# Strassen blocks of keys and queries finished in PSUM, an output in another PSUM ring, weight sums on another engine: a two-layer gated model on one Trainium2 core

## The chip, the core and the metric

The kernel runs on one core of a Trainium2 chip. The metric is device time in microseconds (us). The engines have short names: PE is TensorE (matmuls and transposes), DVE is VectorE, ACT is ScalarE, POOL is GpSimd, and SP issues most of the DMAs. Each engine works through its own instructions in order. All data is float32.

## What is computed

Eight sequences of 256 tokens and 1024 features go through two layers. Each layer is a cross-attention and a feed-forward part, each added to x through a gate:

```python
x = x + tanh(g_xattn[0]) * autocorrelation(layernorm(x), ctx, ctx)
x = x + tanh(g_ffn[0])   * lora_ffn(layernorm(x), ...)      # the LoRA rank is chosen per token
x = x + tanh(g_xattn[1]) * attention(layernorm(x), ctx, ctx, mask, wq, wk, wv, wo)
x = x + tanh(g_ffn[1])   * fourier_ffn(layernorm(x), ...)   # W_base and an update from Fourier coefficients

def rope(x):                       # on queries and keys, 128 features of a head
    x1, x2 = x[..., :64], x[..., 64:]
    return x * cos + concat([-x2, x1]) * sin

def autocorrelation(Q, K, V):      # 8 heads of 128 features
    corr = ifft(fft(q) * conj(fft(k))).real
    w, idx = top_k(corr, int(2 * log(256)));  w = softmax(w)
    return sum(w[i] * v[min(idx[i] + pos, 255)] for i in range(topk))
```

The attention has 32 query heads on 8 key and value heads of 128 features.

## The kernel before

**Passes and stages.** Two passes of four sequences run one after another. A pass has four stages: the first layer's autocorrelation, its LoRA feed-forward part, the second layer's attention and its Fourier feed-forward part. The keys and values of the attention depend on the context alone, so their projection (`keys_values`) runs beside the autocorrelation: the generator `fill` takes its next steps at chosen places, so that PE has matmuls while other engines work on spectra. In the first pass the folding of the last layer's weights stands there too. A scheduler decides the final order on each engine.

**Seven products.** Matrix products are made by the Strassen-Winograd scheme: 7 products of half-size blocks in the order `SEVEN = (1, 2, 6, 7, 4, 5, 3)`, where operands are sums made beforehand (`left_operands`, `right_operands`) and results are combined. For keys, values and queries `combine` (L221 to L257) does that as each product ends in a PSUM tile of 128 x 512: product 1 is copied to `u` by ACT; 2 plus u is the first finished block (L229); 6 is added into u (L232); 7 plus u is `w` (L235); w minus 4 is a block (L254); 5 plus w is a block and 5 is added into u; 3 plus u is the last block (L250). For product 5 there are two forms. With `alone` (queries of the second pass) DVE makes both sums from PSUM (L238, L239). Otherwise ACT copies the product to `m` (L243), and POOL adds it into u (L244) and makes the block (L246). A finished block lies in SBUF: `c` for a key, `qT` for a query, `v` for a value.

**Rope.** A finished key or query is turned by `rope` (L718 to L728): DVE multiplies the two halves crosswise by the sine into a temporary tile (L725, L726), and the whole by the cosine (L727), and POOL adds the two (L728). The temporary tile "rope" has one buffer, so the next rope's first multiply waits for the add. Queries are turned in place; keys go from c into the tile that a DMA writes to the keys in DRAM.

**PSUM rings.** Beside the autocorrelation these are `ps_kv`, two tiles for the products of keys and values; `ps_dft`, four for spectra; one each for the correlation and for `ps_out`. The last holds the two transposes `pt` of a turn and the two outputs `po` (L540), one after another. Each po gets two matmuls (L542) and is added to x by two residuals on DVE (L381). A turn of the autocorrelation (a sequence's half of the features) makes spectra, multiplies them on DVE from PSUM (L438 to L441), adds the products on POOL (L442, L444), finds the largest lags (L584 to L598), and finishes the turn before. POOL makes the next turn's sums of tokens (L471 to L474), after which DVE corrects `ke` (L477). In the attention the query products (L987), the output products (L1017 in the first pass, L1080 in the second) and nothing else share the four tiles of `ps_mm`.

**Attention.** A step is one block of two sequences and one key head with its four query heads. Queries of the next step, scores, values and outputs are interleaved. In the first pass the outputs use seven products (`outputs`, L1017). In its block 1, at each second head, `finer_weights` makes from the weights of two heads the sums that the second pass needs: for each of seven operands two subtractions on DVE (L933, L934), two on POOL (L935, L936), and two DMAs to DRAM, from three buffers of "fine". The second pass takes two heads together (`outputs_of_two`) with 49 quarter-size products; POOL makes their left operands `oI` (L1059), and `stream_wo` loads the weights through a ring of seven big tiles.

**Big tiles.** Three groups of seven tiles of 4 KB per partition, "a", "b" and "xn", are shared by the stages; which of a and b is `ga` and `gb` alternates between passes. `before_fourier` prepares the Fourier part's first operands (norm, transposes, sums) near the end of the attention: six tiles, in ga, which is also the ring of the wo stream. `stored_weight` (L196) places 14 half weights: the first seven in the first group, the others in the second. For the Fourier part these are gb and "xn". The next pass's context blocks `cx` and their sums (POOL, L155 and L159) lie in one of the big groups too.

Of the kernel before, what the change touches and what calls it, by code (L numbers as in the profile page):

```python
# [19 lines left out]
P = 128  # L20
# [26 lines left out]
def flamingo_kernel(ctx: ExitStack, tc: tile.TileContext, a: dict, out: bass.AP):  # L47
# [147 lines left out]

    def stored_weight(groups, where):  # L196

        ops = {}
        for n, r in enumerate(SEVEN):
            ops[r] = Halves([groups[(2 * n + i) // 7] for i in range(2)], f"w_{r}")  # L200
            ops[r].load(where(r))
        return ops

# [14 lines left out]
        eng.tensor_sub(t4, t2, q[1][0])  # L218
        return {1: q[0][0], 2: q[1][0], 3: q[1][1], 4: t4, 5: t1, 6: t2, 7: q[0][1]}

    def combine(r, ps, tiles, new, dest, alone=False):  # L221


        if r == 1:
            tiles["u"] = new("u")
            nc.scalar.copy(tiles["u"], ps)
        elif r == 2:
            c = dest()
            nc.vector.tensor_add(c, ps, tiles["u"])  # L229
            return c, (0, 0)  # L230
        elif r == 6:
            nc.vector.tensor_add(tiles["u"], ps, tiles["u"])  # L232
        elif r == 7:
            tiles["w"] = new("w")
            nc.vector.tensor_add(tiles["w"], ps, tiles["u"])  # L235
        elif r == 5 and alone:
            c = dest()
            nc.vector.tensor_add(c, ps, tiles["w"])  # L238
            nc.vector.tensor_add(tiles["u"], ps, tiles["u"])  # L239
            return c, (1, 1)  # L240
        elif r == 5:
            m = new("m")
            nc.scalar.copy(m, ps)  # L243
            nc.gpsimd.tensor_add(tiles["u"], tiles["u"], m)  # L244
            c = dest()
            nc.gpsimd.tensor_add(c, tiles["w"], m)  # L246
            return c, (1, 1)
        elif r == 3:
            c = dest()
            nc.vector.tensor_add(c, ps, tiles["u"])  # L250
            return c, (0, 1)
        elif r == 4:
            c = dest()
            nc.vector.tensor_sub(c, tiles["w"], ps)  # L254
            return c, (1, 0)
        return None

    def add_product(r, ps, x, g, ng, part):

# [134 lines left out]
    def autocorrelation(p, xt, pools, beside, late):  # L394
# [88 lines left out]
        def turn(this, before, coming):  # L483


            after = None
            if this:
                b, cols, end, qe, qo, ke, ko = this
                if coming:
                    coming = loads(coming)  # L490
                kr_ps, ki_ps = dft((KCE, ke)), dft((KSE, ko), (NYQ, ke))


                kr, ki, kn = sb("kr"), sb("ki"), sb("kn")
                nc.scalar.copy(kr, kr_ps)
                nc.scalar.copy(kn, kr_ps)
                nc.scalar.activation(ki, ki_ps, AF.Copy, scale=pair)
                nc.scalar.copy(kn[0:1, :], ki_ps[0:1, :])
                re, im = sb("re"), sb("im")
                products(spectrum((CE, SE), (qe, qo)), kr, ki, kn, re, im, False)  # L500
                fill(2)

            if this:
                vr_ps, vi_ps = dft((KCO, ko)), dft((KSO, ke))
                vr, vi = sb("vr"), sb("vi")
                nc.scalar.copy(vr, vr_ps)
                nc.scalar.copy(vi, vi_ps)

                nc.vector.scalar_tensor_tensor(
                    kr[0:1, :], end[0:1, :], 2.0 * S, kr[0:1, :], ALU.mult, ALU.add  # L510
                )
                fill((1 if p == 0 else 2) if before else 6 if p == 0 else 2)
            last = not this
            if before:
                if last:
                    fill(3)
                b_cols, b_tiles, (bkr, bki, bkn, bvr, bvi, both) = before

# [12 lines left out]
                products(spectrum((CO, SO), wt[::-1]), bvr, bvi, bvr, odr, odi, True)  # L531
                fill(3 if last else 2)
            if this and coming:
                after = sums(*coming)

            def back(l):


                if before:
                    po = ps_out.tile([P, HALF], F32, tag="out", name="po")  # L540
                    for i, (k, sp) in enumerate(((0, er), (3, odi)) if l else ((1, ei), (2, odr))):
                        nc.tensor.matmul(po, inv2[:, k, :], sp, start=(i == 0), stop=(i == 1))  # L542
                    residual(b_tiles[0][:, b_cols], po, tg_x[0])
                    residual(b_tiles[1][:, b_cols], po, tg_x[0] if l else ntg_x[0])
                    fill(1 - l)

            if last:
                back(0)
                back(1)
                return None, None  # L550
            w = big_tile("xn", [4, S], "w")
            cor = correlation(re, im, 0)
            fill(1)
            back(0)
# [175 lines left out]
    def keys_values(n, groups, pools, tab):  # L730
# [61 lines left out]
        for u in range(4):  # L792
# [4 lines left out]
            for r in SEVEN:  # L797
                ps = ps_kv.tile([P, 2, S], F32, tag="kv", name=f"ps_{kind[1]}")
                for l in range(2):
# [9 lines left out]
                        )  # L809
                    if l == 0:  # L810
                        yield
                out_tile = lambda: w2.tile([P, 2, S], F32, tag="kv", name=kind[1])
                dest = (lambda: new("c")) if kind == "wk" else out_tile
                done = combine(r, ps, tiles, new, dest)
                if done:
                    c, (i, j) = done
                    if kind == "wk":
                        kT = out_tile()
                        rope(kT, c, tab[:, 0, :], tab[:, 1, :], w1)
                        place = kT_d.rearrange("(q l i) p t -> q i p l t", l=2, i=2)  # L820
                        nc.sync.dma_start(
                            place[i_u, i, :, :, t0 + j * S : t0 + (j + 1) * S], kT
                        )
                    else:
                        r0, c0 = t0 + j * S, i_u * HALF + i * S
                        nc.sync.dma_start(
                            v_d[r0 : r0 + S, c0 : c0 + S].rearrange("(t p) d -> p t d", p=P), c
                        )
# [33 lines left out]
    def attention(p, xt, gq, go, keep, norms, xops, ahead):  # L862
        with (
# [59 lines left out]
            def finer_weights(step):  # L923

                blk, g = step
                for n, r in enumerate(SEVEN):
# [3 lines left out]
                        w1.tile([P, 2, 2, S], F32, tag="fine", name=f"fine_{i}", bufs=3)  # L930
                        for i in ("t67", "t45")
                    )
                    nc.vector.tensor_sub(t45[:, 1], q[0][1], q[0][0])  # L933
                    nc.vector.tensor_sub(t67[:, 1], q[1][1], q[0][1])  # L934
                    nc.gpsimd.tensor_sub(t67[:, 0], q[1][1], t45[:, 1])  # L935
                    nc.gpsimd.tensor_sub(t45[:, 0], t67[:, 0], q[1][0])  # L936
                    nc.sync.dma_start(wo2_d[g // 2][:, n, 0], t67)
# [41 lines left out]
            def queries(step, qT):  # L979
# [3 lines left out]
                for r in SEVEN:  # L983
                    ps = ps_mm.tile([P, 2, S], F32, tag="mm", name="ps_q")
                    for l in range(2):
                        for c in range(KH):
# [4 lines left out]
                                start=(c == 0),  # L991
                                stop=(c == KH - 1),
                            )
                    new, dest = (lambda tag: half(tag, 1)), (lambda: half("qT", 7))
                    done = combine(r, ps, tiles, new, dest, paired)
                    if done:
                        qT[done[1]] = done[0]
                        rope(done[0], done[0], tab_q[:, 0, :], tab_q[:, 1, :], w1)
                    yield

            def outputs(step, ops):
# [359 lines left out]
    for p in range(NPASS):  # L1361
# [42 lines left out]
        with tc.tile_pool(name="at_keep", bufs=1, reuse_waits="tile") as kp:  # L1404
# [26 lines left out]
            def before_fourier(ps_t, tag):  # L1431
                norm = norm_stats(xt[:2])
                tiles = []
                for t in range(2):
                    xn = big_tile(ga, [D], "xn")
                    normed(xn, xt[t], *norm, t)
                    tiles.append(big_tile(ga, [KC, P], "xnT"))
                    transposed(tiles[t], xn, ps_t, tag)
                q = [[s[:, k * KH : (k + 1) * KH, :] for k in range(2)] for s in tiles]
                both = big_tile(ga, [2, KH, P], "s12")  # L1440
                s = both[:, 0], both[:, 1], big_tile(ga, [KH, P], "s4")
                first.update(left_operands(nc.vector, q, *s))

            attention(p, xt, gb, ga, keep, norms, xops, before_fourier)
        fourier_ffn(p, xt, (gb, "xn"), first)

# [136 lines left out]
```

## Time and profile before

| | us |
|---|---|
| median of three runs | 3379.02 |
| lowest and highest | 3375.74, 3380.23 |
| the profiled execution's own time | 3388.48 |
| its span | 3386.4 |

The granted TensorE clock is 0.99 over the span. The stages are told by the lines that run in them; cutting the span there gives this table of time, busy time of each engine with the number of instructions, granted clock, DMA share and GB/s:

```profile
core 0: us, PE busy (x) PEld busy (x) DVE busy (x) ACT busy (x) POOL busy (x), PEclk, DMA share, GB/s
0.00:100.00 100.00, 81.71 (x312) 63.99 (x313) 74.18 (x134) 20.06 (x34) 42.35 (x36) 0.95 0.70 257
100.00:395.00 295.00, 281.95 (x1060) 195.32 (x1060) 213.58 (x529) 85.71 (x156) 166.27 (x129) 0.99 0.42 137
395.00:548.00 153.00, 144.51 (x492) 74.70 (x491) 100.30 (x216) 19.79 (x40) 22.33 (x16) 0.97 0.38 139
548.00:1150.00 602.00, 597.74 (x2458) 438.60 (x2457) 460.33 (x725) 163.02 (x438) 247.27 (x234) 1.00 0.40 140
1150.00:1640.00 490.00, 474.51 (x1836) 329.59 (x1835) 363.71 (x572) 133.43 (x350) 280.39 (x240) 0.99 0.50 173
1640.00:1742.00 102.00, 101.42 (x273) 47.35 (x271) 55.00 (x85) 12.67 (x22) 38.11 (x29) 1.00 0.33 119
1742.00:2100.00 358.00, 340.94 (x1320) 248.72 (x1321) 259.39 (x609) 101.03 (x182) 176.59 (x136) 0.97 0.43 141
2100.00:2243.00 143.00, 140.55 (x499) 75.84 (x499) 73.65 (x186) 20.00 (x40) 22.97 (x20) 0.99 0.23 71
2243.00:3284.00 1041.00, 1022.52 (x4954) 889.64 (x4953) 768.33 (x1436) 292.16 (x795) 550.99 (x589) 1.00 0.51 165
3284.00:3386.00 102.00, 97.22 (x263) 45.53 (x261) 45.25 (x68) 10.28 (x18) 23.59 (x19) 0.99 0.10 41
```

From above: the start and the rest of the first pass's autocorrelation with keys and values; its LoRA part; block 0 and block 1 of its attention; its Fourier part; then the four stages of the second pass (autocorrelation with keys and values, LoRA, attention, Fourier). Records of matmuls overlap a little, and their ends are modelled, so a stage's PE time can look fuller than PE is.

In the lists of groups a row reads: line, engine, operation, out<-in by the program's names, shapes, count | busy us, mean ns of one | idle time of the engine just before them with what ended most of it. In the timelines a row reads: start us, duration us, engine, line, operation, out<-in, shapes, count [idle before <-releaser].

### The profile page before, as it was taken

To read this page: it belongs to the slowest core of one execution; us is meant where nothing else is said; L and a number is where in the kernel's file an instruction comes from. 1 tells how busy PE (TensorE), PEld (TensorE's weight loads), DVE (VectorE), ACT (ScalarE), POOL (GpSimd) and SP (SyncE) were. 2 spreads that over 40 slices of the span, in tenths; PEclk is the share of its full clock that TensorE was granted. 3 is DMA by queue.
4 is the path that set the end of the run, shared out by engine and by line. 5 is a ranking of instruction groups with operands and counts; after the bars stand their busy time and mean duration, and the time that the engine had idled before them with its cause. 6 is when DMAs were issued, how large, how long until landed. Compare 5 with 4: busy or idle time off the path is not lost. (4 is left out here: it accounts for less than half of the span.)

```text
span 3386.4 us, 39800 instructions
## 1 busy us (share of the span) xinstructions
PE 3283.1 (97%) x13456; PEld 2409.3 (71%) x13456; DVE 2413.7 (71%) x4553; ACT 858.2 (25%) x2075; POOL 1570.9 (46%) x1445
## 2 busy tenths in 40 slices
PE   8899999999999999999999999999999999999999
PEld 6666556777777766775456767568888888888864
DVE  7787656877777787677648775467777777777773
ACT  1333111322232322222113321113222222222310
POOL 4655212434443465466535552113564554554662
PEclk9999999999999999999999999999999999999999
DMA  7433625333333454564253434043454455555641
GB/s 270 171 116 110 217 96 177 119 135 133 136 128 132 133 204 144 177 225 169 81 196 125 141 105 162 7 157 103 161 183 157 155 167 172 165 165 179 207 140 50
DMA packets 215783, 505.56 MB, mean 149 GB/s; under 512 B 25076, under 2 KB 102900, under 8 KB 215582
## 3 DMA queue, kind: packets, MB, share of 16 engines
q1 hardware_dynamic: 214430, 498.84, 43.7%
q0 software_dynamic: 1152, 4.19, 0.3%
q8 instruction: 107, 1.75, 0.2%
q14 instruction: 94, 0.77, 0.1%
HBM read 394.96 MB, written 108.00 MB: 149 GB/s over the span
## 5 line engine op out<-in xcount | busy, mean ns | idle before, releaser
L728 POOL TENSOR_TENSOR qT<-qT,rope 128x512 f32<-128x512 f32 x128 | 169.5, 1324 | 675.2 <-DVE qT L727 675.2
L987 PE MATMUL ps_q<-xn,wq 128*128 128x256 f32 x1920 | 429.2, 379 | 2.7 <-DVE x L381 2.7
L987 PEld LDWEIGHTS ps_q<-xn,wq 128*128 128x128 f32 x1920 | 364.5, 190 | 54.3 <-DVE x L381 3.9
L1158 ACT ACTIVATE s<-s,nmx 128x256 f32<-128x256 f32 x512 | 255.9, 500 | 351.1 <-DVE nmx L1155 350.3
L1153 DVE COPY_PREDICATED s<-keep,ps_s 128x512 f32<-128x512 uint8 x256 | 185.4, 728 | 147.6 <-PE ps_s L1144 141.5
L987 PE MATMUL ps_q<-xn_t,wq 128*128 128x256 f32 x1280 | 285.6, 379 | 0.0
L987 PEld LDWEIGHTS ps_q<-xn_t,wq 128*128 128x128 f32 x1280 | 243.2, 190 | 33.1
L381 DVE SCALAR_TENSOR_TENSOR x<-po,tg,x 128x512 f32<-128x512 f32 x248 | 178.3, 744 | 121.5 <-PE po L1332 43.5
L1190 PE MATMUL av<-wT,v 128*128 128x256 f32 x1024 | 248.5, 386 | 13.7 <-ACT wT L1185 13.7
L1167 DVE TENSOR_SCALAR s<-s,tot 128x256 f32<-128x256 f32 x512 | 245.7, 520 | 7.1
L1144 PE MATMUL ps_s<-kT,qT 128*128 128x256 f32 x1024 | 249.6, 381 | 0.0
L1190 PEld LDWEIGHTS av<-wT,v 128*128 128x128 f32 x1024 | 193.3, 191 | 68.6 <-ACT wT L1185 24.2
L1080 PE MATMUL po<-wo,oI 128*128 128x256 f32 x896 | 218.6, 383 | 12.4 <-POOL oI L1059 8.3
L1185 ACT COPY wT<-pt 128x512 f32<-128x512 f32 x256 | 138.5, 588 | 361.3 <-PE pt L1179 360.9
L1144 PEld LDWEIGHTS ps_s<-kT,qT 128*128 128x128 f32 x1024 | 193.6, 192 | 26.3 <-issue 0.7
L1017 PE MATMUL po<-wo,oT 128*128 128x512 f32 x448 | 201.8, 593 | 0.0
L1080 PEld LDWEIGHTS po<-wo,oI 128*128 128x128 f32 x896 | 167.6, 191 | 44.8 <-POOL oI L1059 11.8
L1152 POOL MEMSET s<- 128x512 f32 x256 | 128.4, 527 | 141.2 <-PE pt L1179 133.7
L1155 DVE TENSOR_REDUCE nmx<-s 128x2 f32<-128x512 f32 x256 | 174.1, 683 | 6.9
L1080 PE MATMUL po<-wo,oT 128*128 128x256 f32 x672 | 168.7, 381 | 4.0 <-DVE co L1095 2.0
L1198 ACT COPY oT<-av 128x512 f32<-128x512 f32 x128 | 74.9, 585 | 362.9 <-PE av L1190 361.3
L264 POOL TENSOR_TENSOR x<-x,part 128x512 f32<-128x512 f32 x48 | 69.0, 1438 | 206.5 <-ACT part L263 206.4
(296 smaller groups left out, 6519.1 us busy)
## 6 DMA issues: line engine op xcount, KB each, us to landing
wo<-wo_d SPq DMA_DIRECT2D x144, 512.0 KB, 4.6
wq<-in_wq_dram SPq DMA_DIRECT2D x104, 512.0 KB, 3.5
wq<-wq_d SPq DMA_DIRECT2D x96, 512.0 KB, 3.3
wo<-in_wo_dram SPq DMA_DIRECT2D x56, 512.0 KB, 3.9
wo_d<-fine_t SPq DMA_DIRECT2D x56, 512.0 KB, 3.4
wo<-wo_d SPq DMA_DIRECT2D x96, 256.0 KB, 3.4
w<-w_d SPq DMA_DIRECT2D x36, 512.0 KB, 5.4
wo<-in_wo_dram SPq DMA_DIRECT2D x72, 256.0 KB, 3.3
```

What stands on the lines that cost most here:

```text
L381: nc.vector.scalar_tensor_tensor(xs, ps, g, xs, ALU.mult, ALU.add)
L728: nc.gpsimd.tensor_add(dst, dst, t)
L987: nc.tensor.matmul(ps[:, l, :], wops[r][:, l, c, :], xo[r][:, c, :], start=(c == 0), stop=(c == KH - 1),)
L1017: nc.tensor.matmul(po, ops[r][:, h, t * P : (t + 1) * P], wops[r][:, h, :], start=(h == 0), stop=(h == 1),)
L1080: nc.tensor.matmul(po, left[r2][:, h, :], w[:, h, :], start=(h == 0), stop=(h == 1))
L1144: nc.tensor.matmul(ps[:, t, :], qT[i, n][:, l, t * P : (t + 1) * P], kT[:, n * S : (n + 1) * S], start=True, stop=True,)
L1153: nc.vector.copy_predicated(s, keep[b], ps)
L1155: nc.vector.tensor_reduce(nmx, s, AX.X, ALU.max, negate=True)
L1158: nc.scalar.activation(s[:, t, :], s[:, t, :], AF.Exp, bias=nmx[:, t : t + 1], accum_out=tot[:, t : t + 1],)
L1167: nc.vector.tensor_scalar(s[:, t, :], s[:, t, :], tot[:, t : t + 1], None, ALU.mult)
L1185: nc.scalar.copy(wT[i], pt)
L1190: nc.tensor.matmul(av[:, i, :], kv[step][1][:, n * 2 + c, :], wT[i][:, c, :], start=(c == 0), stop=(c == 1),)
```

## The change

1. A finished block of a key or query is written back into the PSUM tile of its product: `combine` gets the tile through `dest(ps)`, and for keys and queries `dest` returns that tile. Rope's three multiplies then read PSUM. A query's result goes into a new `qT` tile; values still go to SBUF.
2. Product 5 has one form: DVE adds it into u, and then makes the block. ACT's copy m and POOL's two additions are gone (32 products: 16 of queries in the first pass, 8 of keys, 8 of values).
3. The autocorrelation's outputs po take tiles of the spectra's ring `ps_dft` instead of `ps_out`.
4. In `finer_weights` the first two subtractions are POOL's too, so all four are.
5. `before_fourier` takes its six tiles from "xn" instead of ga, and the Fourier part's 14 half weights lie in three groups: seven in gb, three in "xn", four in ga. With two groups, as in the LoRA part, the same rule gives the places of before.

```diff
     def stored_weight(groups, where):
         ops = {}
+        place = [groups[0]] * 7 + [groups[1]] * 3 + [groups[-1]] * 4
         for n, r in enumerate(SEVEN):
-            ops[r] = Halves([groups[(2 * n + i) // 7] for i in range(2)], f"w_{r}")
+            ops[r] = Halves(place[2 * n : 2 * n + 2], f"w_{r}")
             ops[r].load(where(r))
         return ops
...
-    def combine(r, ps, tiles, new, dest, alone=False):
+    def combine(r, ps, tiles, new, dest):
         if r == 1:
             tiles["u"] = new("u")
             nc.scalar.copy(tiles["u"], ps)
...
-        elif r == 5 and alone:
-            c = dest()
-            nc.vector.tensor_add(c, ps, tiles["w"])
-            nc.vector.tensor_add(tiles["u"], ps, tiles["u"])
-            return c, (1, 1)
-        elif r == 5:
-            m = new("m")
-            nc.scalar.copy(m, ps)
-            nc.gpsimd.tensor_add(tiles["u"], tiles["u"], m)
-            c = dest()
-            nc.gpsimd.tensor_add(c, tiles["w"], m)
-            return c, (1, 1)
...
+            return None
+        u = tiles["u"]
+        if r == 6:
+            nc.vector.tensor_add(u, ps, u)
+            return None
+        if r == 7:
+            tiles["w"] = new("w")
+            nc.vector.tensor_add(tiles["w"], ps, u)
+            return None
+        if r == 5:
+            nc.vector.tensor_add(u, ps, u)
+        c = dest(ps)
+        if r == 4:
+            nc.vector.tensor_sub(c, tiles["w"], ps)
+        else:
+            nc.vector.tensor_add(c, ps, tiles["w"] if r == 5 else u)
+        return c, {2: (0, 0), 5: (1, 1), 3: (0, 1), 4: (1, 0)}[r]
...
                 if before:
-                    po = ps_out.tile([P, HALF], F32, tag="out", name="po")
+                    po = ps_dft.tile([P, HALF], F32, tag="dft", name="po")
...
-                out_tile = lambda: w2.tile([P, 2, S], F32, tag="kv", name=kind[1])
-                dest = (lambda: new("c")) if kind == "wk" else out_tile
-                done = combine(r, ps, tiles, new, dest)
+                out_tile = lambda _: w2.tile([P, 2, S], F32, tag="kv", name=kind[1])
+                done = combine(r, ps, tiles, new, (lambda ps: ps) if kind == "wk" else out_tile)
...
-                    nc.vector.tensor_sub(t45[:, 1], q[0][1], q[0][0])
-                    nc.vector.tensor_sub(t67[:, 1], q[1][1], q[0][1])
+                    nc.gpsimd.tensor_sub(t45[:, 1], q[0][1], q[0][0])
+                    nc.gpsimd.tensor_sub(t67[:, 1], q[1][1], q[0][1])
...
-                    new, dest = (lambda tag: half(tag, 1)), (lambda: half("qT", 7))
-                    done = combine(r, ps, tiles, new, dest, paired)
+                    done = combine(r, ps, tiles, lambda tag: half(tag, 1), lambda ps: ps)
                     if done:
-                        qT[done[1]] = done[0]
-                        rope(done[0], done[0], tab_q[:, 0, :], tab_q[:, 1, :], w1)
+                        qT[done[1]] = half("qT", 7)
+                        rope(qT[done[1]], done[0], tab_q[:, 0, :], tab_q[:, 1, :], w1)
...
-                    xn = big_tile(ga, [D], "xn")
+                    xn = big_tile("xn", [D], "xn")
                     normed(xn, xt[t], *norm, t)
-                    tiles.append(big_tile(ga, [KC, P], "xnT"))
+                    tiles.append(big_tile("xn", [KC, P], "xnT"))
...
-                both = big_tile(ga, [2, KH, P], "s12")
-                s = both[:, 0], both[:, 1], big_tile(ga, [KH, P], "s4")
+                both = big_tile("xn", [2, KH, P], "s12")
+                s = both[:, 0], both[:, 1], big_tile("xn", [KH, P], "s4")
...
-        fourier_ffn(p, xt, (gb, "xn"), first)
+        fourier_ffn(p, xt, (gb, "xn", ga), first)
```

More of the change, by code (lines that the diff above doesn't have):

```diff
@@ L226, in combine @@
             nc.scalar.copy(tiles["u"], ps)
-        elif r == 2:
-            c = dest()
-            nc.vector.tensor_add(c, ps, tiles["u"])
-            return c, (0, 0)
-        elif r == 6:
-            nc.vector.tensor_add(tiles["u"], ps, tiles["u"])
-        elif r == 7:
-            tiles["w"] = new("w")
-            nc.vector.tensor_add(tiles["w"], ps, tiles["u"])
-        elif r == 5 and alone:
-            c = dest()
-            nc.vector.tensor_add(c, ps, tiles["w"])
-            nc.vector.tensor_add(tiles["u"], ps, tiles["u"])
-            return c, (1, 1)
-        elif r == 5:
-            m = new("m")
-            nc.scalar.copy(m, ps)
-            nc.gpsimd.tensor_add(tiles["u"], tiles["u"], m)
-            c = dest()
-            nc.gpsimd.tensor_add(c, tiles["w"], m)
-            return c, (1, 1)
[L248 to L253, printed above, removed]
+            return None
[4 more added lines that the diff above has]
+        if r == 7:
+            tiles["w"] = new("w")
+            nc.vector.tensor_add(tiles["w"], ps, u)
[4 more added lines that the diff above has]
+        if r == 4:
             nc.vector.tensor_sub(c, tiles["w"], ps)
-            return c, (1, 0)
-        return None
+        else:
+            nc.vector.tensor_add(c, ps, tiles["w"] if r == 5 else u)
+        return c, {2: (0, 0), 5: (1, 1), 3: (0, 1), 4: (1, 0)}[r]
     def add_product(r, ps, x, g, ng, part):
@@ L817, in keys_values @@
                     if kind == "wk":
-                        kT = out_tile()
+                        kT = out_tile(c)
                         rope(kT, c, tab[:, 0, :], tab[:, 1, :], w1)
```

## The prediction

> **What bounds the kernel now.** I read the busy table and the 40 slices first, then the groups of instructions split by shape, then the timelines of the places where TensorE (PE) stood still, and last the chain of waits near the end.
>
> ```profile
> PE 3283.1 (97%) x13456; PEld 2409.3 (71%) x13456; DVE 2413.7 (71%) x4553; ACT 858.2 (25%) x2075; POOL 1570.9 (46%) x1445
> PE   8899999999999999999999999999999999999999
> ```
>
> PE is the bound nearly everywhere, and the change neither adds nor removes a matmul. So only PE's lost time can move. Busy time overstates PE, because the ends of matmuls are modelled: I added up the distances between the starts of matmul records beyond their cadence (216 ns for 256 columns, 429 for 512), which gives about 150 us lost in the span of 3386.4. About 15 of it (400 to 450 us, LoRA weights) has nothing to do with the change. What the change can win lies in some 60 us; what it can lose has no such limit. The profiled execution took 3388.5 us, 9.5 above the median of 3379.0; the sums below come from its trace, and I take their total off the median.
>
> **DVE's cost.** The groups, as line, engine, out<-in, count | busy, mean ns | idle before and its releaser:
>
> ```profile
> L725 DVE TENSOR_TENSOR rope<-c,tab 64x512 f32<-64x512 f32 x32 | 36.0, 1125 | 28.7 <-POOL c L246 23.5 <-POOL k L728 4.1
> L725 DVE TENSOR_TENSOR rope<-qT,tab_q 64x512 f32<-64x512 f32 x128 | 93.0, 727 | 57.8 <-POOL qT L246 50.5 <-POOL qT L728 3.0
> L229 DVE TENSOR_TENSOR qT<-ps_q,u 128x512 f32<-128x512 f32 x32 | 22.1, 690 | 70.8 <-PE ps_q L987 70.8
> L934 DVE TENSOR_TENSOR fine_t<-wo,wo 128x512 f32<-128x512 f32 x28 | 28.5, 1017 | 32.3 <-DMA wo_d<-fine_t 19.0 <-DMA wo<-wo_d 7.6 <-DMA wo<-in_wo_dram 2.7
> L935 POOL TENSOR_TENSOR fine_t<-wo,fine_t 128x512 f32<-128x512 f32 x28 | 44.6, 1592 | 34.4 <-DMA wo<-wo_d 17.3 <-DMA wo_d<-fine_t 17.1
> ```
>
> The 480 rope multiplies (three per block, 160 blocks) took 390.5 us (36.0+29.9+27.9 for keys, 93.0+114.1+89.6 for queries), and one input of each moves from SBUF to PSUM. A rule speaks against that: the Trainium skill (VectorE: DVE Perf Modes, "Rules for kernel authors") says of elementwise work on a matmul's output: accept the slow rate, or copy it to SBUF first if many operations follow; another page (Perfetto Trace Analysis, "Optimizing Scalar/DVE Operations") gives about 125 ns of access on PSUM against 60 on SBUF. By the rule 480 x 0.065 = +31 us (an estimate from that page). The rows say otherwise: PSUM-input adds and multiplies lie at 0.68 to 0.69 us on every line, also beside GpSimd (POOL) work; two-SBUF-input ones reach 0.69 only when POOL rests, and average 0.73 to 1.13. I take the row: 480 x 0.69 = 331, **-59 us**. Added are 64 adds (u and c for 32 r5 products, today on POOL): 64 x 0.69 = **+44**. The 56 finer-weight subtractions leave: **-56.5**. DVE ends near 2342, and the waits for POOL's c (50.5 + 23.5 us) go too.
>
> **POOL's cost.** It loses 64 adds, 44.9 + 41.6 = 86.5 us, and gains 56 subtractions at 1.3 to 1.6 us (rows L246, L935), +73 to +89, all in block 1 of the first attention. ACT loses 32 copies of 588 ns; nothing waited on it for long, worth nothing by itself.
>
> **The hold.** A PSUM tile of a query's or key's block was free after one add of 0.69 us. Now it is held for three multiplies more, +2.07, and r5's for 3.45 in all. Where the ring slot comes round later than that it costs nothing; otherwise PE waits, with POOL no longer in the way. Cost by stage:
>
> **1. Autocorrelation and keys, second pass** (1742 to 2100). First VectorE, then PE:
>
> ```profile
> 1961.49 0.69 DVE L725 TENSOR_TENSOR rope<-c,tab 64x512 f32<-64x512 f32 x1 [2.63 <-POOL c L246]
> ...
> 1967.90 5.15 DVE L725 TENSOR_TENSOR rope<-c,tab 64x512 f32<-64x512 f32 x1
> ...
> 1977.59 0.73 DVE L381 SCALAR_TENSOR_TENSOR x<-po,tg,x 128x512 f32<-128x512 f32 x1
> ```
>
> ```profile
> 1973.25 1.89 PE L807 MATMUL ps_k<-cx,wk 128*128 128x256 f32 x8
> 1979.04 2.08 PE L542 MATMUL po<-re,inv 128*128 128x512 f32 x2 [3.90 <-DVE x L381]
> ```
>
> The second po shares ps_out's one buffer with the first, whose two residuals came late because DVE waited 2.63 us for POOL's c and then lost 4.46 us in a multiply of 5.15. PE lost 4.06 us, and then ran its next records slowly (2.08 for two against 1.02 at 2013), another 2.9. The same at 2023: 3.33 + 2.9. After, the residuals come 2.63 + 4.46 - 1.38 (two adds more) = 5.7 us sooner, and po, in the ring of four spectra, no longer waits for them at all: -13.2. Also gone are 3.2 us at 1922, where v's L250 waited for POOL's u. What is late next: the following turn's query spectra take the slots of the two po and wait for those residuals, behind four spectra of 0.86 us; covered. Against it the hold: ps_kv has two tiles, a product lasts 8 x 0.43 = 3.45 us, and the hold is 2.76 (r2, r4, r3) or 3.45 (r5) with a free DVE, which is busy 259 of 358 us here. Moved under the old DVE times the 32 key blocks of both passes would stall PE 47 us; with the POOL waits gone I put 6 in each pass. Sum -16.4 + 6 = **-10** (-16 to +6).
>
> **2. Start** (0 to 100). PE lost 3.4 us at 48 (a key-weight sum on DVE, behind a rope that waited 3.82 us for POOL's c at 38; less two adds, 2.4 sooner), 1.4 at 80 (the 0.69 add of c behind other DVE work) and 5.5 + 1.4 at 90 (DVE's ke behind POOL's ke, behind POOL's value-weight sums; two r5 adds less stand before them). Won perhaps 12 with slow records, given back 6 by the hold: **-6** (-10 to +4) for the first pass's stage.
>
> **3. First attention, block 0.** ps_mm has four tiles. With the old DVE times the slot of r3 would be 2.4 us late in 7 of its steps; but DVE's wait for POOL's c (50.5 us over 14, 3.6 each) is gone and leaves about 0.3: **+2** (0 to 13).
>
> **4. Block 1** (1150 to 1640), 15 us lost today, most of it where DVE stands before a finer subtraction that waits for a DMA (32.3 us on L934, above) while the softmax waits behind it: 4.2 at 1593, 1.5 and 3.8 after it, 3 x 3.1 earlier. The waits move to POOL; what is queued there is the rope's add L728, behind which the single "rope" tile and so DVE's next rope stand. POOL goes from 280 of 490 us to 280 - 22 + 85 = 343, 70%. That has slack in the mean, little in a burst. **-8** (-18 to +15).
>
> **5. Start of the second pass.**
>
> ```profile
> 1751.01 1.74 DVE L477 SCALAR_TENSOR_TENSOR ke<-end,ke 128x512 f32<-128x512 f32 x1 [8.79 <-POOL ke L471]
> ```
>
> The context's load now waits for a slot that a Fourier weight holds (ga instead of "xn"), and POOL's six context sums (1.3 each, done during the Fourier stage before) come at 1741 to 1749, ahead of ke. DVE stands at L477, with the first key add queued behind it: ke about 1752.6, and with the hold the fourth product near 1757.2 instead of 1753.4. **+5** (0 to +10).
>
> **6. Second attention.** PE loses 1.1 us per pair of steps to POOL:
>
> ```profile
> 2515.22 0.68 DVE L250 TENSOR_TENSOR qT<-ps_q,u 128x512 f32<-128x512 f32 x1
> ...
> 2519.12 0.70 DVE L727 TENSOR_TENSOR qT<-qT,tab_q 128x512 f32<-128x512 f32 x1
> ```
>
> ```profile
> 2519.30 2.10 PE L1080 MATMUL po<-wo,oI 128*128 128x256 f32 x8 [1.12 <-POOL oI L1059]
> ```
>
> Under these times r3's slot (free at 2515.9, in future at 2519.8) is 2.7 late; all such steps together 47 us. But two outputs' adds (0.5 each) and a slow multiply (1.66) stood inside this rope; in the changed order it runs uninterrupted, three times 0.69, and the next transposes fill the gap. The stall stands in the place of POOL's, not beside it: **-2** (-8 to +20).
>
> **7. Its end.** Today the prepared Fourier operands take six of the wo stream's slots, and loads come one behind another:
>
> ```profile
> 3256.85 4.88 DMA wo<-wo_d
> ...
> 3265.59 4.93 DMA wo<-wo_d
> ```
>
> PE lost about 9 us from 3240 to 3288. With those tiles in "xn" the loads run ahead again; 2.6 of it (norm and transposes on DVE) stays. What may be late next are the last Fourier weights, now issued behind the whole stream. **-5** (-8 to +5).
>
> **Sum:** -10 - 6 + 2 - 8 + 5 - 2 - 5 = -24. Median 3379 - 24 = **3355 us**; its own range 3341 to 3371.
>
> **Rivals.**
> (a) *The PSUM hold decides*, slower. Place: ps_kv and r3, r5 in ps_mm. Price moved under the old times: 47 + 24 + 47 = 118 us. Half of it, 59, less the 15 or so in my sum (6 + 6, 2, and the stall of part 6), makes -24 + 44 = +20: 3399; all of it some 3460. It decides once the hold costs over 39 us. For it: DVE is 71% busy and in order. Against: in all the bad places of before DVE was behind because of POOL.
> (b) *Nothing moves*: each gain met by a wait of the next resource, as in part 6: 3379, within 6.
> (c) *POOL becomes late in block 1*: one exposed us in each of 28 finer steps in place of the gain of 8: -24 + 36 = +12, 3391. For it: L935 itself waited 34.4 us for DMAs, and a POOL add is twice a DVE one. Against: 30% of POOL is free there.
> (d) *More is won*, with the hold free everywhere: -24 - 17 = -41, 3338.
>
> Chances: forecast 0.52, (a) 0.20, (b) 0.14, (c) 0.09, (d) 0.05. A measurement of this kernel tells 0.2%, 6.8 us, from no change. Faster: 0.52 + 0.05 = 0.57; same 0.14; slower 0.29. The range to hold 8 in 10: 3338 to 3399.
>
> **What would show it.** Rope multiplies all at 0.69, no wait of them for POOL, DVE near 2340; no stall before L542 in the second pass; PE's time in 1742 to 2100 down by 5 or more; block 1 shorter, with no waits for DMAs on DVE; the last wo loads ahead of need. Waits of L807 and of po for third rope multiplies over 39 us in all, or ropes waiting for POOL's L728 in block 1, would make the prediction wrong.

## The result, and the profile after

| | before | after |
|---|---|---|
| median | 3378.76 us (4 runs) | 3346.86 us (3343.24 to 3351.35, 4 runs) |
| ratio | | 0.9907 (95% interval 0.989 to 0.9925) |
| span of the profiled execution | 3386.4 us | 3349.6 us |

The change made the kernel 31.9 us faster. The forecast was 24. The spans of the two profiled executions differ by 36.8 us: the one of before took 3388.5 us, 9.7 above its median, and the one of after 3351.4, 4.5 above.

The busy table of the changed kernel, and its groups by shape (line, engine, out<-in, count | busy, mean ns | idle before, releaser; lines have moved up by 11 to 13, so rope is L714 to L717 and finer weights L921 to L924):

```profile
PE 3268.8 (98%) x13456; PEld 2408.0 (72%) x13456; DVE 2356.0 (70%) x4561; ACT 844.1 (25%) x2043; POOL 1513.2 (45%) x1437
```

```profile
L714 DVE TENSOR_TENSOR rope<-ps_q,tab_q 64x512 f32<-64x512 f32 x128 | 88.7, 693 | 8.1 <-POOL qT L717 1.3
...
L714 DVE TENSOR_TENSOR rope<-ps_k,tab 64x512 f32<-64x512 f32 x32 | 22.2, 693 | 9.5 <-POOL k L717 8.0
...
L923 POOL TENSOR_TENSOR fine_t<-wo,fine_t 128x512 f32<-128x512 f32 x28 | 36.2, 1292 | 0.0
...
L922 POOL TENSOR_TENSOR fine_t<-wo,wo 128x512 f32<-128x512 f32 x28 | 36.1, 1289 | 19.0 <-DMA wo_d<-fine_t 15.7 <-DMA wo<-in_wo_dram 2.9
```

All 480 rope multiplies now take 0.67 to 0.70 us, the waits for POOL's c (74 us) are gone, and VectorE (DVE) is down 57.7 us, not the 71.6 of the sum. More than the missing 14 us is in one row that the prediction did not look at, the softmax's last multiply, s by 1/tot (before, then after):

```profile
L1167 DVE TENSOR_SCALAR s<-s,tot 128x256 f32<-128x256 f32 x512 | 245.7, 520 | 7.1
L1154 DVE TENSOR_SCALAR s<-s,tot 128x256 f32<-128x256 f32 x512 | 266.1, 560 | 7.5
```

Where the time went. The first record of a stage's first matmuls was read from both traces; the last two columns are the time that each stretch won and the forecast's parts for it:

| first or last record | before | after | won in the stretch | forecast |
|---|---|---|---|---|
| first LoRA product, first pass | 396.8 | 383.3 | 13.5 | 6 (part 2) |
| first query product of block 1 | 1022.9 | 1006.1 | 3.3 | -2 (part 3) |
| first key product, second pass | 1742.3 | 1723.9 | 1.6 | 8 (part 4) |
| last po, second pass | 2099.8 | 2078.3 | 3.1 | 5 (parts 1 and 5) |
| first query product, second pass | 2242.6 | 2217.7 | 3.4 | 0 |
| last score, second pass | 3215.6 | 3182.8 | 7.9 | 2 (part 6) |
| last matmul | 3380.6 | 3343.8 | 4.0 | 5 (part 7) |

The first thing to look for was the stall before the second po. TensorE's (PE's) timeline where it stood at 1979 and 2.08 us for two records followed:

```profile
1967.47 1.89 PE L796 MATMUL ps_k<-cx,wk 128*128 128x256 f32 x8
1969.20 1.02 PE L531 MATMUL po<-re,inv 128*128 128x512 f32 x2
```

No wait, and two records in 1.02 us. But not all is gain. At 1456 three timelines of the changed kernel (DVE, POOL, PE) show something new:

```profile
1456.80 8.12 DVE L1154 TENSOR_SCALAR s<-s,tot 128x256 f32<-128x256 f32 x2
1464.84 0.15 DVE L1152 RECIPROCAL tot<-tot 128x2 f32<-128x2 f32 x1
1465.02 0.62 DVE L1154 TENSOR_SCALAR s<-s,tot 128x256 f32<-128x256 f32 x2
```

```profile
1459.55 1.25 POOL L922 TENSOR_TENSOR fine_t<-wo,wo 128x512 f32<-128x512 f32 x1
1460.77 1.28 POOL L923 TENSOR_TENSOR fine_t<-wo,fine_t 128x512 f32<-128x512 f32 x1
1462.00 1.28 POOL L921 TENSOR_TENSOR fine_t<-wo 128x512 f32<-128x512 f32 x1
1463.23 1.27 POOL L924 TENSOR_TENSOR fine_t<-fine_t,wo 128x512 f32<-128x512 f32 x1
1467.17 1.30 POOL L922 TENSOR_TENSOR fine_t<-wo,wo 128x512 f32<-128x512 f32 x1 [2.67 <-DMA wo_d<-fine_t]
```

```profile
1466.35 1.98 PE L1004 MATMUL po<-wo,oS 128*128 128x512 f32 x4 [2.81 <-DVE x L370]
```

The same pair of multiplies takes 0.62 us eight microseconds later. The first pair ends just after 1464.5, when POOL's unbroken run of additions (from 1453.38) has its first gap; and PE waits for the residual queued behind it. The releaser named is DVE's residual, but what holds it up seems to be POOL. The experiments had to tell whether that run is what the finer subtractions cost, and which edit brought the gain.

### The profile page after: what moved, and what is told of

The parts are those of the page before. It is cut to its first block, busy times and chain, and to the rows that moved or that the text cites. A ratio compares the mean times of both kernels' runs of the same rounds, so it can differ in the third digit from the quotient of the medians.

```text
span 3349.6 us, 39704 instructions
## 1 busy us (share of the span) xinstructions
PE 3268.8 (98%) x13456; PEld 2408.0 (72%) x13456; DVE 2356.0 (70%) x4561; ACT 844.1 (25%) x2043; POOL 1513.2 (45%) x1437
## 5 line engine op out<-in xcount | busy, mean ns | idle before, releaser
L717 POOL TENSOR_TENSOR qT<-qT,rope 128x512 f32<-128x512 f32 x128 | 169.3, 1322 | 671.0 <-DVE qT L716 670.9
L1154 DVE TENSOR_SCALAR s<-s,tot 128x256 f32<-128x256 f32 x512 | 266.1, 560 | 7.5
```

The costliest lines, as they stand in the source:

```text
L717: nc.gpsimd.tensor_add(dst, dst, t)
L1154: nc.vector.tensor_scalar(s[:, t, :], s[:, t, :], tot[:, t : t + 1], None, ALU.mult)
```

## The experiments

Theory "freed VectorE" is mine: the gain comes from product 5 and the blocks in PSUM, which take DVE's waits for POOL away. "Rings and places" gives it to the other edits, "hold" is rival (a). Later "shut out" stands for the picture above and "POOL late" for rival (c). Each run has its own runs of before on its chip. From the intervals, two kernels whose gains differ by less than about 7 us are not told apart by their times; there the stretches of the profiles, one execution of each kernel, have to help.

| run | edits on before | median, before beside it | ratio (95%) |
|---|---|---|---|
| e1_r5_dve | product 5 | 3358.2, 3387.7 | 0.9917 (0.9903 to 0.993) |
| e2_psum_not_r5 | blocks in PSUM, not those of the old product 5 | 3394.1, 3387.7 | 1.0019 (1.001 to 1.0028) |
| e3_r5_and_psum | both | 3346.3, 3387.7 | 0.9881 (0.9866 to 0.9896) |
| e4_po_ring | po's ring | 3396.8, 3387.7 | 1.0026 (1.0017 to 1.0036) |
| e7_after_old_po | all but po's ring | 3357.4, 3390.3 | 0.9908 (0.9892 to 0.9923) |
| e10_e3_fine | both, finer sums | 3358.4, 3390.3 | 0.9911 (0.9896 to 0.9927) |
| e11_e3_places | both, places | 3344.8, 3390.3 | 0.9871 (0.9851 to 0.9891) |
| e12_places_p2 | both, places in the second pass | 3345.0, 3390.3 | 0.9868 (0.9851 to 0.9886) |
| e13_fine_norm_act | e10, multiply by ACT | 3340.2, 3389.9 | 0.9861 (0.9846 to 0.9877) |
| e14_norm_act | e3, multiply by ACT | 3336.6, 3389.9 | 0.9849 (0.9836 to 0.9863) |
| e15_ke_pool | e11, ke off DVE | 3365.3, 3389.9 | 0.9931 (0.9917 to 0.9945) |
| e16_places_norm_act | e11, multiply by ACT | 3331.9, 3387.6 | 0.9835 (0.9819 to 0.9852) |

**Product 5 by DVE.**

```diff
-            m = new("m")
-            nc.scalar.copy(m, ps)
-            nc.gpsimd.tensor_add(tiles["u"], tiles["u"], m)
+            nc.vector.tensor_add(tiles["u"], ps, tiles["u"])
             c = dest()
-            nc.gpsimd.tensor_add(c, tiles["w"], m)
+            nc.vector.tensor_add(c, ps, tiles["w"])
```

> The kernel before with one edit: product 5 is added into u and made into its block by VectorE; finished blocks still go to SBUF. Theory 'freed VectorE' (the gain comes from VectorE no longer waiting for POOL's c, 74 us of waits before): 8 to 16 us faster than before, the stalls before L542 at 1979 and 2023 gone or halved. Theory 'rings and places' (the gain comes from po's ring and the tile places): within 5 us of before. Theory 'hold' (blocks kept in PSUM cost time, which other parts pay back): 15 us faster or more, and faster than the run that also keeps the blocks in PSUM.

29.5 us faster, nearly the whole change's gain, and nearly twice the most that "freed VectorE" gave it (16); "hold" had only a floor of 15. Moving 64 additions to DVE, the busier engine, helped: DVE had waited 74 us for what POOL made of them, and those waits are gone. The edit also makes POOL's queue 64 additions shorter, and no run parts the two effects. In the profiles of the two autocorrelations PE's waits behind DVE fall from 29 us to 23, and those directly behind POOL from 12 to 5. The waits of 3.90 and 3.17 us before the second po in the second pass shrank to one of 1.97; in the first pass a new one of 4.35 stands before a po.

**Blocks in PSUM without it.**

> The kernel before with blocks of keys and queries kept in PSUM and turned from there, save product 5 where it was made by ACT and POOL (first pass's queries, keys, values), which stays as it was. 'Freed VectorE': rope multiplies from PSUM at 0.69 us, the waits for POOL's c stay; 2 to 8 us faster. 'Hold': slower by 3 to 20 us, with waits of the K, V and query matmuls for third rope multiplies. 'Rings and places': within 5 us.

6.4 us slower: "hold" had this one right, "freed VectorE" not. The edit is the changed kernel's, except that blocks which POOL makes stay in SBUF. DVE's wait list and PE's timeline in block 0 of the first attention:

```profile
DVE rope L725 <- POOL qT L246: 52.9, 15, 4.3
DVE rope L725 <- POOL c L246: 24.0, 7, 6.6
```

```profile
667.68 1.96 PE L1019 MATMUL po<-wo_t,oS 128*128 128x512 f32 x4 [1.69 <-DVE qT L727]
```

The waits for POOL are all still there, and now TensorE waits for the third multiply, at 667 and in four later steps of block 0 in the same way (1.7 to 2.0 us each, where the prediction had 2.4 in seven steps under the old DVE times). The profiles also show that the edit costs only where POOL makes product 5: from the first LoRA product to the second pass's first key product it is 19.1 us longer than before, while the second attention, where product 5 was DVE's already, is 8.6 shorter.

**Both.**

> The changed kernel with po back in its own buffer, the two finer subtractions back on VectorE and the old tile places: product 5 by VectorE and blocks in PSUM alone. 'Freed VectorE': 15 to 25 us faster than before, over half of the whole change (32). 'Rings and places': at most 8 us faster. 'Hold': at least 5 us slower than product 5 by VectorE alone.

41.4 us faster: more than the whole change, and than the 15 to 25 of "freed VectorE". So blocks in PSUM cost 6 alone and are worth 12 on top of product 5 (41.4 - 29.5). With product 5 made by DVE nothing slow stands between a product and its last multiply, and the stall at 667 is absent; what is left of the hold in the profile of the changed kernel is 1.1 us at 219, 3.6 at 1788, 0.6 and 0.8 in block 1, a part of 4.5 at 1739, and 4.1 at 78, where a rope first waits 6.4 us for POOL's add of the rope before (there is one temporary tile). "Hold" falls as the deciding cost. Without blocks in PSUM the keys' multiplies stay slow (from e1's groups; 693 ns after):

```profile
L718 DVE TENSOR_TENSOR rope<-c,tab 64x512 f32<-64x512 f32 x32 | 32.0, 1001 | 5.9 <-POOL k L721 4.3
```

**po in the spectra's ring.**

```diff
-                    po = ps_out.tile([P, HALF], F32, tag="out", name="po")
+                    po = ps_dft.tile([P, HALF], F32, tag="dft", name="po")
```

> The kernel before with po in the spectra's ring alone. The second po's waits for the first one's residual (1979 and 2023, 13 us with slow records) can go, but query spectra that take the slots of po wait for late residuals, as the changed kernel shows at 130 (5.2 us before the dft of qo). 'Freed VectorE': 3 to 8 us faster or nothing, since the late residuals themselves stay late. 'Rings and places': 8 to 15 us faster.

9.2 us slower, which neither theory expected. The stall before po is gone, and the next user of the slot has it. The loss is in the first pass, where the stretch up to the first LoRA product is 11.7 us longer than before; the second pass's autocorrelation is 3.2 shorter (PE's timeline, once in each pass):

```profile
141.21 2.04 PE L422 MATMUL dft<-qo,mats 128*128 128x512 f32 x2 [5.65 <-DVE x L381]
...
2039.12 2.08 PE L422 MATMUL dft<-qo,mats 128*128 128x512 f32 x2 [5.18 <-DVE x L381]
```

The prediction called this wait covered by four spectra. It is not, as long as the residuals themselves are late. The other way round, the changed kernel without this edit:

> The changed kernel with po back in its own buffer; finer subtractions by POOL and the new places stay. Product 5 by VectorE with blocks in PSUM alone was 41 us faster than before, the whole change 32, so the other three edits cost some 9. Theory 'ring': po in the spectra's ring costs it (it cost 9 alone): 38 to 43 us faster than before, no wait before the dft of qo at 130. Theory 'places': the late start of the second pass costs it: 31 to 36 us faster.

32.9 us faster, ratio 0.9908 against 0.9907 with the edit. "Ring" falls; the number fits "places", but the runs of the places below do not bear that out. So the ring costs nothing measurable once DVE is on time, and brings nothing: in the first pass the wait of 3.4 us before po at 125 merely becomes one of 5.0 before qo at 130. The 9.5 us that are lost between "both" and the whole change lie elsewhere.

**Finer sums by POOL, on top of both.**

> Product 5 by VectorE and blocks in PSUM, and the finer subtractions by POOL. Block 1 of the first attention loses 14 us around its end without this edit and 20 in the changed kernel. 'POOL late': 2 to 8 us slower than without the edit, 34 to 39 us faster than before, with POOL's rope adds or sums as releasers at the end of block 1. 'VectorE freed' (my forecast gave it 8 us): 44 to 50 us faster than before.

31.9 us faster against 41.4: the edit costs some 9.5, more than either theory gave, and my forecast had it win 8. The pair e7 (above) and e11 (below), which differ in this edit alone and ran on one chip, gives 12.7 (32.9 against 45.5). DVE, POOL and PE of e10:

```profile
1190.27 8.35 DVE L1153 TENSOR_SCALAR s<-s,tot 128x256 f32<-128x256 f32 x2
```

```profile
1196.88 1.33 POOL L923 TENSOR_TENSOR fine_t<-fine_t,wo 128x512 f32<-128x512 f32 x1
1200.90 1.29 POOL L921 TENSOR_TENSOR fine_t<-wo,wo 128x512 f32<-128x512 f32 x1 [2.69 <-DMA wo_d<-fine_t]
```

```profile
1200.06 3.61 PE L1003 MATMUL po<-wo,oS 128*128 128x512 f32 x4 [3.04 <-DVE x L369]
```

Four such multiplies of 8 us stand at 1190, 1327, 1463 and 1575, each followed by a stall of PE of 3 to 4 us. With the subtractions on DVE the longest is 2.35 us. (The whole change's profile has two of the four.) What the forecast counted on is there too: three waits of 1.4 to 2.0 us that PE has in e3 at 1215, 1350 and 1482 are gone. The new stalls, with slow records behind them, outweigh it: from block 1's first query product to the second pass's first key product, e3 takes 716.7 us and e10 728.4. The rope adds on POOL are not late: DVE's ropes wait 9.4 us for them in all, 10.2 without the edit.

**The new places, in both passes and in the second.**

> Product 5 by VectorE and blocks in PSUM, and the new places in both passes. 'Places' cost: the second pass starts 4 to 8 us later (loads of context behind Fourier weights, POOL's context sums ahead of ke), the end of the second attention wins 2 to 5: 36 to 41 us faster than before. My forecast's account (+5 at the start, -5 at the end): as without the edit, 41, within 3.

> Product 5 by VectorE and blocks in PSUM, and the new places in the second pass alone, where no pass follows. If the places cost at the start of the second pass and pay at the end of the second attention, this keeps the second alone: 2 to 5 us faster than product 5 and blocks in PSUM alone, 43 to 47 faster than before. If the late loads were covered at the end anyway: the same, 41.

45.5 and 45.3 us faster: not told apart from each other, nor clearly from 41.4 without them. The profiles show both sides of the forecast's account. From the last score to the end e3 wins 0.7 us against before, e11 4.2. This side is firm: the stretch is 159.1 to 161.0 us in the six profiles with the new places in the second pass, and 163.5 to 165.1 in the eight without. At the start of the second pass the first four key products take 1.1 us longer than before in e3, 5.9 in e11. But e12, with the old places there, takes 5.1 longer as well, for another reason: POOL's ke, behind its context sums in e11, waits for a load in e12 (POOL of e12):

```profile
1727.47 1.26 POOL L460 TENSOR_TENSOR ke<-cn 128x512 f32<-128x512 f32 x1 [6.03 <-DMA cn<-in_ctx_dram]
```

That load lands 6 to 9 us after the first key product in the runs with the old places, so it covers part of what the new ones cost, and how much differs from run to run.

**The multiply that POOL shuts out, moved to ACT.**

```diff
-                        nc.vector.tensor_scalar(
-                            s[:, t, :], s[:, t, :], tot[:, t : t + 1], None, ALU.mult
+                        nc.scalar.activation(
+                            s[:, t, :], s[:, t, :], AF.Copy, scale=tot[:, t : t + 1]
                         )
```

> The run with product 5, blocks in PSUM and finer subtractions by POOL (32 us faster than before), and the softmax's last multiply (s by 1/tot) on ACT instead of VectorE. Theory 'shut out': the finer sums cost 10 us because VectorE's two multiplies, 0.35 us each when POOL rests, stood 8 us at 1190, 1327, 1463 and 1575 until POOL's run of additions ended; without an operation that POOL can shut out there the stalls of 3.2 us after them go, and 38 us or more are won against before, within 4 us of the same edit without the finer subtractions on POOL. Rival 'POOL late': POOL's queue is late with rope adds and sums of the residual; the stalls stay, and the kernel stays 8 us or more behind the one whose finer subtractions are VectorE's.

> Product 5 and blocks in PSUM alone (41 us faster than before), and the softmax's last multiply on ACT. 'Shut out': the multiplies took 1.2 to 2.3 us in some 40 places here; 2 to 6 us are won, 43 to 48 against before. 'POOL late': nothing, or a loss of up to 10 us, since ACT's multiply of a row block takes longer than VectorE's 0.35 and comes before the transposes.

49.7 us with the finer sums on POOL (17.8 more than without this edit), and 53.3 with them on DVE (11.9 more, above both theories). The cost of the finer sums falls from 9.5 to 3.6, within the 4 that "shut out" gave. By the times alone that fall is within the noise; the profiles bear it out, since in the stretch from block 1's first query product to the second pass's first key product the finer sums cost 11.7 us with the multiply on DVE, and 3.3 with it on ACT (710.4 against 707.1). "POOL late" falls: POOL still has the same additions, and the stalls at 1200, 1336 and 1473 are gone. In e13, DVE in the middle of POOL's run of additions from 1187 to 1198 shows what is not shut out, residuals with one input in PSUM and one in SBUF, four in 2.71 us. The second row is the group of the moved multiplies:

```profile
1192.31 2.71 DVE L369 SCALAR_TENSOR_TENSOR x<-po,tg,x 128x512 f32<-128x512 f32 x4
```

```profile
L1153 ACT ACTIVATE s<-s,tot 128x256 f32<-128x256 f32 x512 | 230.0, 497 | 36.3 <-DVE tot L1151 36.3
```

**ke off DVE.** DVE stands 66 us in all before ke's correction, waiting for POOL.

```diff
-            nc.vector.scalar_tensor_tensor(ke, end, -2.0, ke, ALU.mult, ALU.add)
+            twice = one("twice")
+            nc.scalar.activation(twice, end, AF.Copy, scale=-2.0)
+            nc.gpsimd.tensor_add(ke, ke, twice)
```

> Product 5, blocks in PSUM and the new places (45 us faster than before), and ke's correction off VectorE: ACT makes -2 x end, POOL adds it. VectorE waits 66 us for POOL's ke in the changed kernel with key adds queued behind it, and the correction, with two inputs in SBUF, took up to 6.6 us beside a run of POOL. 'Shut out': the stalls at 1735 (4.9) and 1903 (1.6) shrink, 3 to 9 us won, 48 to 54 against before. 'POOL late': POOL has 16 adds more ahead of its products, 0 to 5 us lost.

A miss: it lost 21 us against e11 (45.5 to 24.6), by the profiles in the two autocorrelations. The group, and a wait of ACT that it caused, with PE's place there:

```profile
L467 ACT ACTIVATE twice<-end 128x512 f32<-128x512 f32 x16 | 10.1, 629 | 94.7 <-DMA end<-in_ctx_dram 52.5 <-POOL ke L468 42.2
```

```profile
1922.31 0.63 ACT L467 ACTIVATE twice<-end 128x512 f32<-128x512 f32 x1 [9.72 <-POOL ke L468]
1922.84 0.57 ACT L516 COPY wt<-pt 128x512 f32<-128x512 f32 x1
```

```profile
1923.56 1.09 PE L514 MATMUL pt<-ident,both 128*128 128x128 f32 x4 [5.97 <-POOL cx_t L159]
```

The new tile has one buffer, so ACT waits for POOL's add of the turn before, and the copies that free PE's transposes stand behind it. The wait was moved, not removed. A second buffer, or a later place in ACT's order, was not tried.

**Put together.**

> The version that the runs point to: product 5 by VectorE, blocks in PSUM and the new places, with po's own buffer and the finer subtractions on VectorE as before, and the softmax's last multiply on ACT. The two parts were worth 45 and, against product 5 and blocks alone, 12 us more; added up 53 to 57 us faster than before. If the places' gain at the end of the second attention is taken by another wait: 50 to 53, as without them.

55.6 us faster than before, ratio 0.9835: faster than both kernels of this study, though not told apart from e14 (0.9849). VectorE is busy 64% of the span instead of 71.

## Why the prediction was right

**Right.** Taking POOL out of the way of DVE was the lever; e1 and e3 show it, though not how much of it is DVE's waits and how much POOL's shorter queue. Row against rule: rope from PSUM took 0.69 us, as the row of PSUM additions said, and the estimate of +31 us from access figures did not come. Rival (a) is excluded at the size that it needed: over 39 us of hold, against stalls of 10 to 15 us in all. The account of the places, +5 at the start and -5 at the end, came out as +6.8 for the first four key products and -4.0 at the end, though e12 showed that the start can be late without them. At the start the context sums and the correction of ke do stand before the first key add, as said (DVE, then PE, of the changed kernel; the PE row's "issue" ends as the third rope multiply, 1738.22 + 0.69, does):

```profile
1734.43 1.74 DVE L466 SCALAR_TENSOR_TENSOR ke<-end,ke 128x512 f32<-128x512 f32 x1 [10.62 <-POOL ke L460]
...
1738.22 0.69 DVE L716 TENSOR_TENSOR k<-ps_k,tab 128x512 f32<-128x512 f32 x1
```

```profile
1739.01 6.52 PE L796 MATMUL ps_k<-cx,wk 128*128 128x256 f32 x16 [4.52 <-issue]
```

At the end the chain of waits has no DMA left, as forecast: PE's output products run 23.42 us in one piece where three loads of weights stood before.

```profile
3219.58 0.86 PE po L1319 x2
3220.44 23.42 PE po L1067 x108
3243.86 3.43 PE po L1319 x8
```

**Terms that were mis-sized.** The hold was not among them: some 5 us in the first pass's stage and 4 to 8 in the second's, for 6 and 6, and 1.4 in block 1 in place of 2 in block 0. Too small was what product 5 and blocks win: 41 us in place of the 16 of parts 1, 2, 3 and 6 (10 + 6 - 2 + 2). Part 2 (13.5 for 6) and part 3 (3.3 for -2) came out beyond their own ranges. So the sum is near in part by luck: these surpluses met part 4, which had the wrong sign. In the second attention the rope runs uninterrupted as part 6 said, and PE then waits 0.33 behind a transpose where it waited 1.12 for POOL. A part of the surplus, 1.95 us at 2106, is a DMA of LoRA weights that was late before and is not after; nobody forecast it.

**A line that was misread.** Part 1 put the 3.2 us at 1922 down to v's L250, waiting for POOL's u. In the profile of before, u was done at 1917.5, and DVE stood in ke's correction until 1921.7:

```profile
1912.60 9.07 DVE L477 SCALAR_TENSOR_TENSOR ke<-end,ke 128x512 f32<-128x512 f32 x1 [7.98 <-POOL ke L471]
```

So what broke part 4 could be seen before the change, beside a run of POOL that ended at 1921.1. That stall is not gone, as part 1 had it: in the changed kernel it is 6.35 us, at 1912 (last section).

**The step that failed: part 4.** It counted the DMA waits that leave DVE's queue, and POOL's load in the mean (343 of 490 us), and had -8; the edit costs 9.5. It put at nothing what POOL's additions do to DVE's operations beside them, though the prediction had seen it on the ropes. POOL was not late. The cost is on the other engine: POOL's longer run of additions holds up a DVE multiply, 8 us in place of 0.35. Rival (c) had the sign and not the mechanism. In the changed kernel's own profile, with two of the four long multiplies, the edit costs less: its stretch is 1.0 us longer than e3's and 2.6 longer than e11's (e7 6.3 over e11, e10 11.7 over e3), so that with the other edits' gain 1.6 us were still won there. That profile is 11 us longer than e3's, and its second pass's autocorrelation alone is 12 us longer; there the late start and ke's correction (last section) stand.

**A step that was unnecessary: po's ring.** Part 1 gave the removed wait two reasons, residuals 5.7 us sooner, and the ring. The first suffices (e3 has no such stall in the second pass, with po in its old buffer). The second alone costs 9.2, since the spectra that take the slots are not covered. Part 1's 10 us came out as 15.3 in e3 from the second pass's first key product to its last po, in one profile; this stretch is 342 to 356 us in the runs with both edits (e15 apart), for a reason that the last section gives in part.

## What to carry to other kernels

Count what an engine waits for in order before you count its busy time: work moved to the busier engine won 29 us, since that engine had been waiting for it, and the other one's queue became shorter. Holding a PSUM tile for three more operations costs only what stands between them: a net gain of 12 us while its engine is on time, a net loss of 6 us with a slow partner in the chain. When work moves to GpSimd, look not only at its queue but at which VectorE operations then stand beside an unbroken run of it, and give those another engine or an operand in PSUM; both kept their time here.

## What was not expected of the hardware

A DVE operation beside POOL's additions can stand still for the rest of their run, not for one instruction. Seen here: a multiply by a scalar from SBUF to SBUF, 0.35 us when POOL rests, up to 8.09; a multiply of two SBUF tiles, 0.69 up to 5.15; and ke's correction, two SBUF inputs, 0.69 up to 9.07 (before) and 6.62 (in the changed kernel at 1904, with a stall of PE behind it):

```profile
1904.62 6.62 DVE L466 SCALAR_TENSOR_TENSOR ke<-end,ke 128x512 f32<-128x512 f32 x1 [7.98 <-POOL ke L460]
```

```profile
1912.50 3.42 PE L796 MATMUL ps_k<-cx,wk 128*128 128x256 f32 x8 [6.35 <-DVE v L244]
```

In e3, e10 and e11 the same one took 1.74, with POOL's run beside it too and a stall of 1.5 us in place of 6.35; in e7, e12, e13, e14 and e16 it took 6.62 again. No edit separates the two groups, so what decides who gets in stays open. It is part of why single profiles differ in this stretch: 342 to 347 us in the first group, 350 to 356 in the second, with the changed kernel. Even the fastest kernel, e16, still has this stall. Operations with an input in PSUM and at most one in SBUF, ropes and residuals, kept their time. The Trainium skill (SBUF — State Buffer, "Who interferes with whom") says why this pair of engines can meet: a copy or multiply by a scalar that uses both of VectorE's ports, or an operation with two SBUF inputs, shares a port pair with GpSimd, which is held for a whole instruction. The runs agree with which operations are hit, but show waits over some seven POOL instructions in a row (e10 at 1190); that it is a port is the page's word, and no run here shows it.
